# Deformable products of a convolution block: a PSUM bank of the general ring for each half band, in place of a bank of their own

## The chip, the cores and the metric

One core of one Trainium2 chip. The metric is the device time of one execution, in microseconds (us). Engines: TensorE (PE, with its weight loads PEld), VectorE (DVE), ScalarE (ACT), GpSimd (POOL) and SyncE (SP). TensorE writes only to PSUM, which this kernel uses as eight banks of 512 fp32 numbers per partition. Each engine works through its own queue in the order that the compiler wrote; an instruction that waits for a semaphore holds all that stand behind it.

## The reference, cut to what matters

Two layers run on 32 images of 96 channels, 56 x 56, all in fp32.

```python
# layer 0: inverted residual
h = silu(bn(conv1x1(x, w1)))             # 96 -> 576
h = silu(bn(depthwise3x3(h, w2)))
s = squeeze_excite(h)
x = x + bn(conv1x1(h * s, w3))           # 576 -> 96
# layer 1
ca, sa = ...                             # gates from |rfft2(x)|, channel sums
y = x * ca * sa
aux = concat([y, coord, resized |rfft2(y)|])
offset = conv3x3(aux, off_w)             # 9 taps, 2 numbers each
gate = sigmoid(conv1x1(relu(conv3x3(aux, dg1_w)), dg2_w))
y_base = conv3x3(y, base_w)
sampled = bilinear samples of y at 9 shifted points of each pixel
y_def = einsum('bcthw,oct->bohw', sampled, def_w) + def_b
z = (1 - gate) * y_base + gate * y_def
out = relu(batch_norm(z) + x)            # statistics over all images
```

## The kernel before

All weights stay on the chip. The hidden layer of one image, the attention (two spectra by matrix products) of the next, and the deformable convolution of a third are interleaved. The deformable part sets the pace: it goes by bands of 8 rows (7 bands an image, 224 in all), each band in two halves of 28 columns, and the function `layers` writes the three streams into one list of steps. A counter `slot` advances at each `pump()`, 17 slots a band. The streams `second` (attention) and `first` (hidden layer) are advanced in proportion to the slots, and the list `later` holds closures with the slot at which they are due. A scheduler then orders each engine's instructions from this program (SP's order is the program's own), and it also decides which buffer of a pool each tile gets and whose release it has to wait for.

One half of a band, in its order: `sample_tiles` forms the samples by matmuls (L739) from transposed blocks `yt` and from weights `wc`; ACT copies them to `v` (L743) and `pack` moves part of them (L750). Three slots into the next half, `end_half` calls `deform`, which sums seven products per half (L758) into PSUM. `weights` multiplies `wc` by `wr` on DVE (L710), both loaded by DMA through SP. `block_channels` makes `yt`: POOL copies blocks (L721), PE transposes them (L725), ACT copies them out (L727).

Before, both halves of a band go into one bank `pd`, from a pool of one buffer. Two slots after the second half `join` calls `combine`, four DVE operations on the whole band: L797 reads `pd` into `z` (with the bias added and the base convolution `yb` subtracted), L798 and L799 blend with the gate, L800 takes the statistics. Seven slots later `store` writes `z` to memory through POOL's queue (L1061). The pool of `z` has two buffers.

All other matmul results go to banks of the ring `mm`, six buffers, by `bank(p)`: the expansion of the hidden layer (L169, read by ACT L173), the projection (L329, L335), the spectra (L396 and L420; DVE reads squares from the ring in L379), the joint convolution of offsets, gate and base (L615, read by ACT L635, L637 and by DVE L664 into `at`), the rest of the base convolution (L644), the gate (L781), the transposes (L725) and the samples (L739). Small matrices of the attention (L440 and others) go to a bank `acc`. On DVE the hidden layer's depthwise taps (L260, L262, one instruction per tap on a half image) take most of the time; it also weights the rows that are loaded for the deformable part (L602) and reduces the spectra (L437).

```python
# L965
pools(tc, ctx, p, PSUM, (("mm", 6), ("acc", 1), ("pd", 1)))
```

Of the kernel before, what the change touches and what calls it, by code (L numbers as in the profile page):

```python
# [7 lines left out]
FP = mybir.dt.float32  # L8
I32 = mybir.dt.int32
AF = mybir.ActivationFunctionType  # L10
ALU = mybir.AluOpType
AX = mybir.AxisListType
PSUM = bass.MemoryType.PSUM
# [3 lines left out]
C, H, W = 96, 56, 56  # L17
# [3 lines left out]
RB = 8  # L21
# [14 lines left out]
BW = NBW  # L36
# [81 lines left out]
def bank(p):  # L118
    return p["mm"].tile([128, 512], FP, name="mm")


def hidden_constants(tc, ctx, a, p):

    nc = tc.nc
    cp = ctx.enter_context(tc.tile_pool(name="l0c", bufs=1))
    w = p["w0"] = {}
    for name, shape in (("w1", [C, HID]), ("w2", [128, NCH, 9]), ("w3", [128, NCH, C])):
        w[name] = cp.tile(shape, FP, name=name)
        nc.sync.dma_start(w[name], a[name + "L"])
    for name in ("sew1", "seb1", "sew2", "seb2"):  # L130
        w[name] = cp.tile(list(a[name].shape), FP, name=name)
        nc.scalar.dma_start(w[name], a[name])
    for name, parts in (("w1", C), ("w2", 128), ("w3", 128)):
        with tc.tile_pool(name=f"fq{name}", bufs=1) as tp:
            fake_quant(nc, tp, w[name], parts, name)
    with tc.tile_pool(name="l0v", bufs=1) as tp:
        vec = tp.tile([128, 8, NCH], FP, name="vec")
        nc.scalar.dma_start(vec, a["hidvec"])
        vec3 = tp.tile([C, 4], FP, name="vec3")
        nc.scalar.dma_start(vec3, a["bn3"])  # L140
        for n, v in ((1, vec[:, :4]), (2, vec[:, 4:]), (3, vec3.unsqueeze(2))):
            inv, sh = bn_affine(nc, tp, v[:, 0], v[:, 1], v[:, 2], v[:, 3], n)
            for key, t in ((f"inv{n}", inv), (f"sh{n}", sh)):
                w[key] = cp.tile(list(t.shape), FP, name=key)
                nc.vector.tensor_copy(w[key], t)

    p["hp"] = [cp.tile([128, HH + 2, WP], FP, name=f"hp{i}") for i in range(2)]
    for t in p["hp"]:
        nc.gpsimd.memset(t, 0.0)
    p["n_hp"] = 0  # L150
# [458 lines left out]
def conv3(nc, out, weights, yp, channels, j):  # L609

    view = out.rearrange("p (h w) -> p h w", h=RB)
    for k in range(NTAP):
        dy, dx = divmod(k, 3)
        r0 = j * RB + dy + PD - 1
        nc.tensor.matmul(view, weights[:, k], yp[:channels, r0 : r0 + RB, dx + PD - 1 : dx + PD - 1 + W],  # L615
                         start=(k == 0), stop=(k == NTAP - 1))
# [135 lines left out]

def deform(nc, p, pd, v, h):

    out = pd[:C, :BW].rearrange("c (q w) -> c q w", q=RB)[:, :, h * W // 2 : (h + 1) * W // 2]
    for k in range(KA):
        ks = slice(0, 128 if k else C)
        nc.tensor.matmul(out.rearrange("c q (t x) -> c t q x", x=TS), p["w"]["def"][ks, k],  # L758
                         v[ks, k].rearrange("c t s (r x) -> c t (s r) x", r=TS),
                         start=(k == 0), stop=(k == KA - 1))  # L760


def gate_of(nc, p, hid):

    pg = bank(p)
    nc.tensor.matmul(pg[:C, :BW], p["w"]["dg2"], hid, start=True, stop=True)
    return gate_from(nc, p, pg)


def gate_from(nc, p, pg):  # L770
    gate = p["q1"].tile([C, BW], FP, name="gate")
    nc.scalar.activation(gate, pg[:C, :BW], AF.Tanh, bias=p["w"]["half"]("dg2_b", C), scale=0.5)
    return gate
# [11 lines left out]
def base_conv(nc, p, j, yp):  # L785

    pb = bank(p)
    conv3(nc, pb[:C, :BW], p["w"]["base"], yp, C, j)
    yb = p["q1"].tile([C, BW], FP, name="yb")
    nc.scalar.activation(yb, pb[:C, :BW], AF.Identity, bias=p["w"]["cv"]("base_b"))  # L790
    return yb


def combine(nc, p, j, pd, yb, gate, st):

    z = p["q2"].tile([C, BW], FP, name="z")
    nc.vector.scalar_tensor_tensor(z, pd[:C, :BW], p["w"]["cv"]("def_b"), yb, ALU.add, ALU.subtract)  # L797
    nc.vector.scalar_tensor_tensor(z, gate, 1.0, z, ALU.add, ALU.mult)  # L798
    nc.vector.scalar_tensor_tensor(z, z, 0.5, yb, ALU.mult, ALU.add)  # L799
    nc.vector.bn_stats(st[:, j], z)  # L800
    return z
# [146 lines left out]
def pools(tc, ctx, p, space, sizes):  # L948
    for name, bufs in sizes:
        kw = {"space": space} if space else {}  # L950
        p[name] = ctx.enter_context(tc.tile_pool(name=f"l1{name}", bufs=bufs, **kw))


def layers(tc, a, dp, x1d, zd, stats, far):
# [6 lines left out]
    nc = tc.nc  # L961
    B = x1d.shape[0]
    with ExitStack() as ctx:
        p = {"tc": tc, "dp": ctx.enter_context(tc.tile_pool(name="l1d", bufs=3, space=DRAM))}
        pools(tc, ctx, p, PSUM, (("mm", 6), ("acc", 1), ("pd", 1)))  # L965
        hidden_constants(tc, ctx, a, p)
        constants(tc, ctx, a, p)
        yp, = padded(nc, p, a, 1)
# [21 lines left out]
        streams, later = [], []  # L990
        slot = 0
# [68 lines left out]
        def store(b, j, z):  # L1060
            nc.gpsimd.dma_start(zd[b][:, j * BW : (j + 1) * BW], z)  # L1061

        def join(n, pd, gate, st):
            b, j = bands[n]
            z = combine(nc, p, j, pd, ybs[n], gate, st)
            later.append((slot + 7, lambda: store(b, j, z)))
            if j == NBD - 1:
                nc.vector.bn_aggr(stats[:, b], st)

        def end_half(n, h, v, gate, st):  # L1070
            if h == 0:
                pds[n] = p["pd"].tile([128, 512], FP, name="pd")
            deform(nc, p, pds[n], v, h)
            if h:
                pd = pds.pop(n)
                later.append((slot + 2, lambda: join(n, pd, gate, st)))

        ends, pds = [], {}

        def fill():  # L1080
            for r in range(RB, H + 1, RB):
# [7 lines left out]
        hids, gates, ybs, hds, ready = [], [], [], [], []  # L1089
# [31 lines left out]
        for n, (b, j) in enumerate(bands):  # L1121
            if j == 0:
                st = p["st"].tile([C, NBD, 6], FP, name="st")
# [7 lines left out]
            for h in range(2):  # L1131
                v = p["vp"].tile([128, NTAP, NTH, 2, TP], FP, name="v")
# [19 lines left out]
                if h == 0:  # L1152
                    if n % 2 == 0:
                        gates.extend(gates_of(nc, p, hids[n // 2]))
                    gate = gates.pop(0)
# [108 lines left out]
def gather_block(tc, a, dp, x1d, zd, stats):  # L1264

    nc = tc.nc
    B = x1d.shape[0]
    sd = dp.tile([B, C, 2], FP, name="sd")
    with ExitStack() as ctx:
        p = {"dp": ctx.enter_context(tc.tile_pool(name="l1d", bufs=1, space=DRAM))}  # L1270
        pools(tc, ctx, p, PSUM, (("mm", 7), ("acc", 1)))
        constants(tc, ctx, a, p, True)
        yp, = padded(nc, p, a, 1)
        table = dp.tile([TAB, 4 * C], FP, name="table")
        with tc.tile_pool(name="l1z", bufs=1) as zp:
            zt = zp.tile([116, TAB * C // 116], FP, name="zt")
            nc.gpsimd.memset(zt, 0.0)
            tz = table.rearrange("(p n) f -> p (n f)", p=116)
            for i in range(4):
                nc.sync.dma_start(tz[:, i * zt.shape[1] : (i + 1) * zt.shape[1]], zt)  # L1280
        pools(tc, ctx, p, None, (("ca", 1), ("s1p", 1), ("xc", 2), ("sp", 1), ("sq", 2), ("hq", 1), ("q1", 2), ("q2", 2),
                                 ("hid", 2), ("off", 1), ("ix", 2), ("vp", 1), ("gp", 4), ("smp", 2)))
        with tc.For_i(0, B, 1) as b:
            st = p["sp"].tile([C, NBD, 6], FP, name="st")
            zo = p["dp"].tile([C, HW], FP, name="zo")
            xi = p["dp"].tile([C, HW], FP, name="xi")
            nc.sync.dma_start(xi.unsqueeze(0), x1d[bass.ds(b, 1)])
            for _ in attend(tc, p, 0, None, None, None, xi, True):
                pass
            for q in range(NB):  # L1290
                attend_table(nc, p, yp, table, xi, q)
            load_freq(nc, p, yp, 0, 0, H)
            for j in range(NBD):
                hid, wq, idx = locate(nc, p, yp, j)
                v = p["vp"].tile([C, NTAP, BW], FP, name="v")
                for t in range(GT):
                    sample_table(nc, p, table, wq, idx, v, t)
                pd = bank(p)
                for k in range(NTAP):
                    nc.tensor.matmul(pd[:C, :BW], p["w"]["def"][:, k], v[:, k], start=(k == 0), stop=(k == NTAP - 1))  # L1300
                z = combine(nc, p, j, pd, base_conv(nc, p, j, yp), gate_of(nc, p, hid), st)
                nc.sync.dma_start(zo[:, j * BW : (j + 1) * BW], z)
            mv = p["sp"].tile([C, 2], FP, name="mv")
            nc.vector.bn_aggr(mv, st)
            nc.sync.dma_start(zd[bass.ds(b, 1)], zo.unsqueeze(0))
            nc.sync.dma_start(sd[bass.ds(b, 1)].rearrange("o c n -> (o c) n"), mv)
    nc.sync.dma_start(stats, sd.rearrange("b c s -> c b s"))
# [209 lines left out]
```

## Time and profile before

| | |
|---|---|
| time, median of 3 runs | 9049.27 us (9045.97 to 9068.44) |
| the profiled execution | 9059.03 us, of which the profile's span is 9057.2 us |
| mean granted TensorE clock | 0.939 of full speed |
| busy: PE, PEld | 8175.3 us (90%), 5193.5 us (57%) |
| busy: DVE, ACT, POOL | 7184.4 us (79%), 5393.5 us (60%), 2902.8 us (32%) |
| DMA | 163 GB/s over the span |

Times of single instructions and of waits come from the profiled execution. A line of a group gives: source line, engine, operation, tiles written and read, shapes, count; then busy us and mean ns of one; then the idle time of the engine just before these instructions, and what ended it. A line of the waits gives: engine and line that waited, what released it, us in total, times, the longest. A line of the timeline gives start, duration, engine, line, operation, count and, in brackets, the idle time before it with its releaser. A fp32 matmul appears as two records. The last 280 us or so, a normalisation that waits for DMA, have no matmuls.

### The profile page before, as it was taken

The numbers are of one execution on the slowest core, as the hardware profiler recorded it, in microseconds if no ns is written. First come the engines' busy times: TensorE is split into PE (matmuls) and PEld (weight loads), VectorE is DVE, ScalarE is ACT, GpSimd is POOL, SyncE is SP. The second block draws the span as 40 slices with busy tenths as digits, with TensorE's granted clock in tenths as the row PEclk, the third lists the DMA queues.
The fourth block names the chain that finished last, engine by engine and source line by source line (L and its number), as shares of the span: only waits on it lengthen the run. The fifth ranks groups of instructions, "written<-read, shape, count | busy, mean of one in ns | idle before, by whom it ended". The sixth has DMA issues, their size and how long they took to land. (4 is left out here: it accounts for less than half of the span.)

```text
span 9057.2 us, 137476 instructions
## 1 busy us (share of the span) xinstructions
PE 8175.3 (90%) x52406; PEld 5193.5 (57%) x52406; DVE 7184.4 (79%) x6629; ACT 5393.5 (60%) x10486; POOL 2902.8 (32%) x2800
## 2 busy tenths in 40 slices
PE   5889999999999999999999999999999999999960
PEld 3456565665656566565656656565665655566640
DVE  7688888888888888888888888888888888888333
ACT  2356665666666666666666666666666666666553
POOL 0233333333333333333333333333333333333210
PEclk9889999999999999999999999999999999999985
DMA  2356666666666666666666666666666666666669
GB/s 82 108 142 160 163 169 165 157 154 153 163 166 171 166 157 147 158 165 164 172 161 154 159 157 168 165 174 161 154 154 160 165 166 172 166 156 144 144 188 416
DMA packets 1068758, 1486.48 MB, mean 164 GB/s; under 512 B 590191, under 2 KB 839839, under 8 KB 1055807
## 3 DMA queue, kind: packets, MB, share of 16 engines
q1 hardware_dynamic: 858995, 985.20, 46.4%
q10 hardware_dynamic: 153803, 329.80, 10.2%
q0 software_dynamic: 55296, 162.60, 6.7%
q8 instruction: 420, 6.88, 0.4%
q14 instruction: 244, 1.99, 0.1%
HBM read 1064.29 MB, written 412.65 MB: 163 GB/s over the span
## 5 line engine op out<-in xcount | busy, mean ns | idle before, releaser
L262 DVE SCALAR_TENSOR_TENSOR acch<-hp,w,acch 128x1512 f32<-128x1512 f32 (+1 forms) x2250 | 4456.4, 1981 | 141.4 <-ACT hp L173 103.8
L615 PE MATMUL mm<-yp,c_jointW 104*128 104x448 f32 x4032 | 1679.6, 568 | 10.1 <-DMA yp<-fqd 10.1
L758 PE MATMUL pd<-v,c_def 128*96 128x224 f32 (+1 forms) x6272 | 1468.8, 382 | 142.7 <-DVE z L797 115.6
L721 POOL COPY ybl<-yp 96x448 f32<-96x448 f32 x896 | 1048.3, 1198 | 1204.9 <-PE mm L725 1204.8
L758 PEld LDWEIGHTS pd<-v,c_def 128*96 128x96 f32 (+1 forms) x6272 | 1062.2, 176 | 449.8 <-issue 116.9
L615 PEld LDWEIGHTS mm<-yp,c_jointW 104*128 104x128 f32 x4032 | 776.6, 196 | 784.2 <-issue 747.4
L743 ACT COPY v<-mm 96x288 f32<-96x288 f32 (+1 forms) x2688 | 1004.3, 441 | 156.0 <-PE mm L739 109.3
L169 PE MATMUL mm<-xt,w 96*128 96x392 f32 (+3 forms) x2688 | 1058.5, 527 | 35.3 <-DMA xt<-in_x 33.1
L739 PE MATMUL mm<-wc,yt 64*96 64x144 f32 x12544 | 1056.9, 300 | 20.8 <-DVE sq L379 6.7
L739 PEld LDWEIGHTS mm<-wc,yt 64*96 64x96 f32 x12544 | 834.2, 164 | 317.3 <-issue 199.1
L173 ACT ACTIVATE hp<-mm,sh,inv 128x392 f32<-128x392 f32 (+2 forms) x1216 | 810.7, 673 | 344.8 <-PE mm L169 290.5
L710 DVE TENSOR_TENSOR wc<-wc,wr 128x1008 f32<-128x1008 f32 x448 | 566.6, 1265 | 412.5 <-DMA wr<-hd 385.1
L644 PE MATMUL mm<-yp,c_base0W 96*64 96x224 f32 x8064 | 830.1, 358 | 5.7 <-ACT hp L173 5.7
L329 PE MATMUL mm<-hq,w3s 128*96 128x392 f32 x2048 | 749.7, 510 | 63.6 <-DMA hq<-h2d 62.2
L672 POOL DMA_DIRECT2D od<-at x224 | 186.7, 834 | 1908.3 <-DVE at L664 1292.6
L750 ACT COPY v<-v 32x448 f32<-32x448 f32 x1344 | 755.1, 562 | 29.7
L727 ACT COPY yt<-mm 128x384 f32<-128x384 f32 (+1 forms) x896 | 353.9, 439 | 700.7 <-PE mm L725 699.0
L644 PEld LDWEIGHTS mm<-yp,c_base0W 96*64 96x64 f32 x8064 | 555.2, 135 | 282.7 <-issue 61.0
L635 ACT ACTIVATE hid<-mm,c_dg1b 50x448 f32<-50x448 f32 x224 | 140.8, 628 | 868.4 <-PE mm L615 858.4
L476 POOL TENSOR_TENSOR o<-o,xc 96x392 f32<-96x392 f32 x256 | 376.2, 1470 | 806.2 <-ACT o L339 804.2
L222 ACT ACTIVATE acch<-acch,sh,inv 128x1568 f32<-128x1568 f32 x288 | 488.4, 1696 | 202.8 <-DVE acch L262 176.5
L329 PEld LDWEIGHTS mm<-hq,w3s 128*96 128x96 f32 x2048 | 323.0, 166 | 395.2 <-issue 367.5
(194 smaller groups left out, 9325.3 us busy)
## 6 DMA issues: line engine op xcount, KB each, us to landing
h2d<-acch ACTq DMA_DIRECT2D x288, 784.0 KB
wc<-hd SPq DMA_DIRECT2D x896, 252.0 KB
wr<-hd SPq DMA_DIRECT2D x448, 504.0 KB
hq<-h2d SPq DMA_DIRECT2D x128, 980.0 KB
hq<-h2d SPq DMA_DIRECT2D x128, 784.0 KB
hq<-x1d SPq DMA_DIRECT2D x768, 98.0 KB
ht<-od SPq DMA_DIRECT2D x224, 252.0 KB
hd<-ho ACTq DMA_DIRECT2D x224, 252.0 KB
```

The lines of the kernel that those rows point to most:

```text
L169: nc.tensor.matmul(pt[p0 : p0 + w1.shape[1], : rows * W], w1, xts[hf][:, r0 * W : (r0 + rows) * W], start=True, stop=True)
L173: nc.scalar.activation(h1[lo:hi, row0 : row0 + rows, 1 : 1 + W], pt[lo:hi, : rows * W].rearrange("p (h w) -> p h w", h=rows), AF.Silu, bia ...
L262: nc.vector.scalar_tensor_tensor(acc[:, lo:hi], win, wk, acc[:, lo:hi], ALU.mult, ALU.add)
L329: nc.tensor.matmul(pts[half][:C, :EW], w3s[:, ch], hq, start=(i == 0), stop=False)
L615: nc.tensor.matmul(view, weights[:, k], yp[:channels, r0 : r0 + RB, dx + PD - 1 : dx + PD - 1 + W], start=(k == 0), stop=(k == NTAP - 1))
L644: nc.tensor.matmul(pb[i * BC : (i + 1) * BC, : BW // 2].rearrange("p (h w) -> p h w", h=RB // 2), w["base"][:, k], yp[:C, r0 + i * RB // 2 ...
L710: p["tc"].keep_in_program_order(nc.vector.tensor_tensor(wc, wc, wr, ALU.mult))
L721: nc.gpsimd.tensor_copy(yb[:, :, s], blocks)
L739: nc.tensor.matmul(pt[k][:C, (t - lo) * KP : (t - lo + 1) * KP], yt[ps, t], s[ps, t * KP : (t + 1) * KP], start=True, stop=True)
L743: nc.scalar.copy(v[:C, :, lo:hi, k].rearrange("c k t p -> c t k p"), pt[k][:C, : (hi - lo) * KP].rearrange("c (t k p) -> c t k p", t=hi - ...
L750: nc.scalar.copy(v[C:, 1 + 2 * i : 3 + 2 * i], v[i * QC : (i + 1) * QC, KA:])
L758: nc.tensor.matmul(out.rearrange("c q (t x) -> c t q x", x=TS), p["w"]["def"][ks, k], v[ks, k].rearrange("c t s (r x) -> c t (s r) x", r=T ...
```

## The change

Each half of a band gets a bank of its own from the ring, and the pool `pd` is gone; the ring has seven buffers. The half's products lie in the first 224 columns of that bank. Two slots after each half's products (before: after the second half's) `difference` reads it into the half's columns of `z`, so L797 is executed twice a band, on 96 x 224 elements as 8 rows of 28. The tile `z` is taken from its pool when the first half is summed. After the second half `combine` does the other three operations on the whole band as before. The fallback `gather_block`, which runs only where offsets reach too far, gets the same operation written out in its old form.

```diff
 def deform(nc, p, pd, v, h):
-    out = pd[:C, :BW].rearrange("c (q w) -> c q w", q=RB)[:, :, h * W // 2 : (h + 1) * W // 2]
+    out = pd[:C, : BW // 2].rearrange("c (q w) -> c q w", q=RB)
...
-def combine(nc, p, j, pd, yb, gate, st):
-    z = p["q2"].tile([C, BW], FP, name="z")
-    nc.vector.scalar_tensor_tensor(z, pd[:C, :BW], p["w"]["cv"]("def_b"), yb, ALU.add, ALU.subtract)
+def difference(nc, p, h, pd, yb, z):
+    half = lambda t: t.rearrange("c (q w) -> c q w", q=RB)[:, :, h * W // 2 : (h + 1) * W // 2]
+    nc.vector.scalar_tensor_tensor(half(z), pd[:C, : BW // 2].rearrange("c (q w) -> c q w", q=RB), p["w"]["cv"]("def_b"),
+                                   half(yb), ALU.add, ALU.subtract)
+
+def combine(nc, p, j, z, yb, gate, st):
     nc.vector.scalar_tensor_tensor(z, gate, 1.0, z, ALU.add, ALU.mult)
     nc.vector.scalar_tensor_tensor(z, z, 0.5, yb, ALU.mult, ALU.add)
     nc.vector.bn_stats(st[:, j], z)
...
-        pools(tc, ctx, p, PSUM, (("mm", 6), ("acc", 1), ("pd", 1)))
+        pools(tc, ctx, p, PSUM, (("mm", 7), ("acc", 1)))
...
-        def join(n, pd, gate, st):
+        def join(n, h, pd, z, gate, st):
             b, j = bands[n]
-            z = combine(nc, p, j, pd, ybs[n], gate, st)
+            difference(nc, p, h, pd, ybs[n], z)
+            if not h:
+                return
+            combine(nc, p, j, z, ybs[n], gate, st)
             later.append((slot + 7, lambda: store(b, j, z)))
...
         def end_half(n, h, v, gate, st):
+            pd = bank(p)
+            deform(nc, p, pd, v, h)
             if h == 0:
-                pds[n] = p["pd"].tile([128, 512], FP, name="pd")
-            deform(nc, p, pds[n], v, h)
-            if h:
-                pd = pds.pop(n)
-                later.append((slot + 2, lambda: join(n, pd, gate, st)))
-        ends, pds = [], {}
+                zs[n] = p["q2"].tile([C, BW], FP, name="z")
+            z = zs.pop(n) if h else zs[n]
+            later.append((slot + 2, lambda: join(n, h, pd, z, gate, st)))
+        ends, zs = [], {}
```

## The prediction, made before the changed kernel ran

> **What bounds the kernel now.** I read the page's engine line and slices first, then busy time by stage, then the waits, then the timeline at the waits that matter. One image takes about 266 us in the steady part; this is the stage line of one image, 3960 to 4227 us (busy time of PE, PEld, DVE, ACT, POOL, then the granted clock):
>
> ```profile
> PE 8175.3 (90%) x52406; PEld 5193.5 (57%) x52406; DVE 7184.4 (79%) x6629; ACT 5393.5 (60%) x10486; POOL 2902.8 (32%) x2800
> 3960.00:4227.00 267.00, 251.99 (x1627) 160.07 (x1626) 223.66 (x198) 165.72 (x325) 90.33 (x88) 0.96 0.65 160
> ```
>
> PE is busy for 252 of 267 us, DVE for 224. So PE sets the time, and what lengthens it is its idle time (15 us an image) and the half-rate clock. Matmuls stand in one queue in compiled order: a wait of one holds all. The waits over the whole run say what ends that idle time:
>
> ```profile
> PE pd L758 <- DVE z L797: 115.6, 26, 6.1
> PE acc L440 <- DVE m_fy L437: 72.8, 30, 5.6
> PE acc L440 <- DVE m_fe L437: 71.1, 31, 2.5
> PE mm L725 <- DVE at L664: 57.2, 28, 5.7
> ```
>
> The first is the one that the change speaks of: the deformable products (L758) wait until VectorE has read `pd`. It happens once an image, at its last band. DVE's and PE's timelines there:
>
> ```profile
> 3956.58 1.53 DVE L710 TENSOR_TENSOR wc<-wc,wr 128x1008 f32<-128x1008 f32 x1 [3.47 <-DMA wr<-hd]
> 3958.03 6.09 DVE L262 SCALAR_TENSOR_TENSOR acch<-hp,w,acch 128x1568 f32<-128x1568 f32 x3
> 3964.15 0.68 DVE L797 SCALAR_TENSOR_TENSOR z<-pd,c_cvec,yb 96x448 f32<-96x448 f32 x1
> ...
> 3959.21 0.93 PE L169 MATMUL mm<-xt,w 96*128 96x392 f32 x2
> 3964.98 1.03 PE L758 MATMUL pd<-v,c_def 96*96 96x224 f32 x2 [4.84 <-DVE z L797]
> ```
>
> DVE lost 3.47 us to a weight transfer, then ran three tap operations of the other image, and only then came to `z`. The read is late because DVE's own queue is late, not because it is long. The clock after such a wait (the last figures of a stage line are clock, DMA share, GB/s):
>
> ```profile
> 3960.00:3966.00 6.00, 1.16 (x5) 0.82 (x5) 5.80 (x7) 3.89 (x8) 0.58 (x1) 0.80 0.98 283
> 3966.00:3972.00 6.00, 6.00 (x22) 4.63 (x21) 4.42 (x7) 1.27 (x3) 1.58 (x3) 0.50 1.05 192
> ```
>
> Between 500 and 8500 us the trace has 115 half-rate stretches, 737 us together (6.4 us each, so 3.2 us of PE work lost each). 32 of them, 232 us, follow a wait of L758.
>
> **Part 1: one DVE read becomes two.** Rows of DVE operations with a PSUM or short operand:
>
> ```profile
> L797 DVE SCALAR_TENSOR_TENSOR z<-pd,c_cvec,yb 96x448 f32<-96x448 f32 x224 | 152.2, 679 | 170.3 <-PE pd L758 166.1
> L922 DVE SCALAR_TENSOR_TENSOR thT<-shift,c_svec,thT 56x56 f32<-56x56 f32 x42 | 10.9, 259 | 0.0
> ```
>
> A line through 56 elements at 259 ns and 448 at 679 gives 439 ns for 224. Two halves cost 878 ns, +199 ns a band, x224 = +45 us of DVE. It is bounded by 0 and by 2 x 679 - 679 = 152 us. DVE idles some 43 us an image, so this is hidden as work; without that cover it would be the whole +45. Matmul count and sizes (7 a half, 379 ns a pass), ACT, POOL and SP lists are the same: no cost. The `z` buffer is taken 12 slots earlier and so waits for the store of two bands before; set against the trace that store lands at least 9 us before, mostly 43 us: nothing. The gather branch, also edited, has no instruction in the trace: nothing.
>
> **Part 2: the wait that goes.** With no `pd` buffer, L758 no longer waits for L797: at most 115.6 us of idle time, plus half of 232 us at half rate = 116.
>
> **Part 3: what is late next.** The half's bank now belongs to the ring, and stays taken from the products until DVE reaches the half: two slots and then DVE's lag. Whichever matmul is compiled onto that bank next waits for DVE, and everything behind it in PE's queue waits too. I took the compiled order of the changed kernel with its waits, and gave each instruction the time that its twin has in the trace of before (the half: the end of the DVE instruction ahead of it, plus 0.44 us). The wait is DVE's time less PE's arrival. The same reckoning on the kernel before gives 357 us between 500 and 8500 us, with 122 us for L758 against 115.6 in the whole run by the profile, so the method reads the old waits rightly. For the changed kernel, by place within an image (us from its end; 30 images):
>
> - Image end: L758's wait does not vanish. The second gate matmul (L781), or a sampling matmul (L739), some three groups ahead of L758, now takes the bank of that same late half. PE meets it about 2 us earlier, DVE is no earlier. 122 becomes 171: +50.
> - At 37: matmuls that take banks DVE reads in L379 and in a half; about 2.6 us an image = 81 when waits that follow at once are counted once. In the order L440 (m_fe, at 54) now stands behind three matmuls of L615, and its 68 us go. With 11 of before: about 0.
> - At 112 to 123, in the second transform: 256, where before has 6: +250. This is the largest. Its mechanism in one image: L169 at 4082.29 takes the bank of a first half that stands in DVE's queue behind the first L262 of the next unit:
>
> ```profile
> 4082.29 0.93 PE L169 MATMUL mm<-xt,w 96*128 96x448 f32 x2
> ...
> 4086.96 1.03 DVE L260 TENSOR_SCALAR acch<-hp,w 128x1568 f32<-128x1568 f32 x1
> 4088.02 3.93 DVE L262 SCALAR_TENSOR_TENSOR acch<-hp,w,acch 128x1568 f32<-128x1568 f32 x1
> ```
>
>  The half would end at 4092.4: L169, and the FFT matmuls behind it, wait 9.9 us. Before, DVE's lag here cost nothing, as no bank hung on it. Alternate images have 5 to 7 and 7 to 13 us.
> - At 145 to 160 (L725 on `at`, L440 on m_fy): 135 becomes 125; as PE arrives late from the place before, the `at` part (53) mostly goes: -50.
> - At 189 and 231 (projection and sampling matmuls behind w3s, a half, and a half behind a wc that waits for DMA): 141, before 3. I take half, +70, because DVE's wait there is for a transfer that a later PE also moves.
>
> Of the 250 I take 205: the transfer wait of L602 (1.4 us an image) is not PE's to repeat. Idle time: 50 + 0 + 205 - 50 + 70 = +275. Bounds: with every wait kept in full 905 - 357 = +548; if waits within 40 us of each other absorb each other fully, 499 - 291 = +208.
>
> Clock: the places at 123 (30 images) and 231 (15) are new waits of over 2 us; 37 takes the place of 54, the image end stays. 45 stretches x 3.2 us = +145. Bounds: 11 more waits over 1.5 us (absorbed) and 63 (full), times 737 / 94 waits x 1/2 = 3.9 us: +43 and +246.
>
> [...] The trace: 28 waits for m_fe, of about 2.4 us, are each followed by half rate, 154 us together. [...]
>
> Sum: 275 + 145 = +420. The profiled execution took 9059.0 us (span 9057.2), 9.8 above the median of 9049.3: 9059 + 420 = 9479 as profiled, 9470 as a median. What lies within 0.3% (27 us) of before I count as no change.
>
> **The rivals.**
> A (my forecast, 0.70): waits move onto the ring and mostly add; 9250 to 9700.
> B (faster, 0.05): no ring matmul meets a late half, since DVE, with halves offered earlier, is ahead of PE. Then 115.6 + 116 are gained: 9049 - 232 = 8817. It decides if the lag at 123 falls below zero from 9.9 and 5.4 us. Against it: DVE's queue has the same operations before the half, and 45 us more.
> C (slower, little, 0.13): a stall early in an image lets DVE catch up, so later ones shrink below my bound: half of the +208, 104, plus 43: about 9200. For it: DVE has 43 us of idle time an image. Against it: much of that idle time is DVE waiting for ACT's hp, which PE feeds, so DVE stops as well when PE stops.
> D (slower, much, 0.10): all add: 548 + 246: 9843.
> E (no change, 0.02): C's losses equal B's gain.
>
> The range 9220 to 9750 holds A, and the near ends of C and D. Faster 0.05, same 0.02, slower 0.93.
>
> **What would show it.** Right: no L758 on L797; new rows of PE waiting for L797 at L169, L396, L739 and L781, 350 to 650 us together; more half-rate time, a mean clock of 0.92 to 0.93 against 0.939; PE's busy time up by the clock alone; L797 448 times at about 440 ns. Wrong: PE's waits for z below 150 us in all, or DVE with no idle time left (then it has become the bound, and Part 1's cover is gone).

## The result and the profile after

The changed kernel takes 9450.61 us (median of 4 runs, 9422.1 to 9474.71) against 9051.45 us for the kernel before on the same chip (4 runs): a ratio of 1.0436, with a 95% interval of 1.0401 to 1.0472. The forecast was 9470 us. Its profiled execution, from which the lines below come, took 9422.1 us.

The head of the page of the changed kernel; the second line gives busy time, share of the span and instructions:

```profile
span 9420.3 us, 137589 instructions
...
PE 8320.5 (88%) x52406; PEld 5277.8 (56%) x52406; DVE 7108.3 (75%) x6853; ACT 5399.9 (57%) x10486; POOL 3029.6 (32%) x2800
```

The number of matmuls is the same (52406 records in either trace, all of which write PSUM tiles: `mm`, `acc` and, before, `pd`), yet PE is busy 145 us longer: the mean granted clock fell from 0.939 to 0.924. The other part is idle time. Between the first and the last matmul record TensorE is idle 551 us before and 769 us after, +218. 145 + 218 = 363 us, which is the growth of the span (9057.2 to 9420.3). DVE, with 224 more instructions, is busy a little less. So nothing here is more work: the loss is waiting and the clock that the waiting costs.

The waits of PE in the changed kernel (us in total, times, longest), its largest eight without two that come once a run:

```profile
PE mm L615 <- DMA yp<-fqd: 149.8, 30, 6.3
PE mm L739 <- DVE z L797: 127.9, 31, 6.7
PE acc L440 <- DVE m_fe L437: 71.6, 32, 3.7
PE mm L169 <- DVE z L797: 67.4, 29, 6.2
PE mm L781 <- DVE z L797: 64.0, 13, 7.0
...
PE mm L725 <- POOL ybl L721: 37.4, 11, 5.2
PE mm L329 <- DMA hq<-h2d: 37.2, 16, 4.7
PE mm L396 <- DVE z L797: 36.1, 14, 3.9
```

Three things are to be read in it. L758 no longer waits for `z` (115.6 us before, 0.8 us now). In its place L739, L169, L781, L396 and, with 15 us in smaller lines, L615, L420 and L329 do: 310 us together. And the first line is new in size: L615 waits 149.8 us for the row of the spectrum (`fqd` to `yp`), 10.1 us before. Against that L440's wait for `m_fy` (72.8 us before) has only 6.8 us left, and L725's for `at` (57.2 us) is gone.

One of the waits for a half, in the timeline (start, duration, engine, line, operation, count, in brackets the idle time before it). First TensorE:

```profile
3794.35 2.81 PE L758 MATMUL mm<-v,c_def 96*96 96x224 f32 x14
...
3799.68 0.99 PE L781 MATMUL mm<-hid,dg2p 50*96 50x448 f32 x2
3807.72 1.06 PE L781 MATMUL mm<-hid,dg2p 50*96 50x448 f32 x1 [7.05 <-DVE z L797]
```

and VectorE in the same stretch:

```profile
3800.24 1.41 DVE L710 TENSOR_TENSOR wc<-wc,wr 128x1008 f32<-128x1008 f32 x1 [4.70 <-DMA wr<-hd]
3801.57 5.61 DVE L262 SCALAR_TENSOR_TENSOR acch<-hp,w,acch 128x1568 f32<-128x1568 f32 x3
3807.22 0.45 DVE L797 SCALAR_TENSOR_TENSOR z<-mm,c_cvec,yb 96x224 f32<-96x224 f32 x1
```

The products were done at about 3797. VectorE had first lost 4.70 us to a weight transfer and then ran three taps of the other image that stand ahead of the read in its queue. The gate matmul, which has nothing to do with that half, took the next turn of its bank and waited 7.05 us; so did all behind it (no matmul record begins between the L781 at 3799.68, which took 0.99 us, and the one at 3807.72). This is the picture of the prediction's first example with another matmul in the place of L758. Counted by time alone, 107 idle stretches of TensorE over 0.5 us, 350 us together, ended within 0.3 us of the end of an L797; VectorE was busy for 301 us of them, 215 in L262 and 47 in the reads themselves.

The new wait of L615 has another cause. The same place in one image, before:

```profile
3051.35 0.41 PE L582 MATMUL acc<-fy,c_rows 29*56 29x56 f32 x4
3051.79 4.57 PE L758 MATMUL pd<-v,c_def 96*96 96x224 f32 x14
...
3058.98 2.73 PE L758 MATMUL pd<-v,c_def 96*96 96x224 f32 x12 [0.40 <-ACT v L743]
3061.86 1.38 PE L615 MATMUL mm<-yp,c_jointW 104*128 104x448 f32 x3 [0.15 <-DMA yp<-fqd]
```

and after:

```profile
3128.13 0.41 PE L582 MATMUL acc<-fy,c_rows 29*56 29x56 f32 x4
3128.47 2.89 PE L758 MATMUL mm<-v,c_def 96*96 96x224 f32 x14
...
3138.19 9.06 PE L615 MATMUL mm<-yp,c_jointW 104*128 104x448 f32 x18 [4.61 <-DMA yp<-fqd]
```

L582 makes the row; ACT copies it, POOL's queue writes it to memory, SP's queue loads it into `yp`; then L615 can start. From the end of L582 to the start of L615 the median is 10.5 us before and 10.4 us after. Before, TensorE had work for that time: fourteen records of L758, for the most part at half rate (4.57 us here at a mean granted clock of 0.63; 4.74 us at 0.63 are the medians over the images), and, ahead of L615, twelve more, six of the seven products of the next half. That second half already had its bank. In the changed kernel it needs one of the ring, whose turn comes after L615's, and the compiled order has all seven products behind L615. Twelve records of cover (2.7 us) are gone, the first fourteen run at full rate (2.89 instead of 4.57 us, a granted clock of 1.00), and what is left of the chain shows as a wait. The fourteen traces divide in this way. Where the second half has its bank early (the kernel before with or without the tap, the split read, the whole band in the ring, and banks of their own), nearly every image has 26 or 28 records of L758 between L582 and L615, and the wait is 1 to 38 us in all. Where each half takes a bank of the ring, it has 14, and the wait is 116 to 150 us, or 61 and 90 us in the two kernels that load an old row.

### The profile page after: what moved, and what is told of

It reads as the page before. It is cut to its first block, busy times and chain, and to the rows that moved or that the text cites. A ratio compares the mean times of both kernels' runs of the same rounds, so it can differ in the third digit from the quotient of the medians.

```text
span 9420.3 us, 137589 instructions
## 1 busy us (share of the span) xinstructions
PE 8320.5 (88%) x52406; PEld 5277.8 (56%) x52406; DVE 7108.3 (75%) x6853; ACT 5399.9 (57%) x10486; POOL 3029.6 (32%) x2800
## 5 line engine op out<-in xcount | busy, mean ns | idle before, releaser
L262 DVE SCALAR_TENSOR_TENSOR acch<-hp,w,acch 128x1512 f32<-128x1512 f32 (+1 forms) x2250 | 4355.6, 1936 | 127.6 <-ACT hp L173 96.9
L615 PE MATMUL mm<-yp,c_jointW 104*128 104x448 f32 x4032 | 1748.3, 585 | 164.6 <-DMA yp<-fqd 149.8
L721 POOL COPY ybl<-yp 96x448 f32<-96x448 f32 x896 | 1177.7, 1341 | 1608.0 <-PE mm L725 1607.9
L758 PE MATMUL mm<-v,c_def 128*96 128x224 f32 (+1 forms) x6272 | 1386.8, 370 | 20.3 <-ACT v L750 17.9
L615 PEld LDWEIGHTS mm<-yp,c_jointW 104*128 104x128 f32 x4032 | 797.4, 203 | 955.5 <-issue 768.9
L739 PE MATMUL mm<-wc,yt 64*96 64x144 f32 x12544 | 1120.7, 304 | 146.5 <-DVE z L797 127.9
L758 PEld LDWEIGHTS mm<-v,c_def 128*96 128x96 f32 (+1 forms) x6272 | 1034.6, 170 | 322.3 <-issue 84.1
L169 PE MATMUL mm<-xt,w 96*128 96x392 f32 (+3 forms) x2688 | 1089.9, 540 | 100.5 <-DVE z L797 67.4
L739 PEld LDWEIGHTS mm<-wc,yt 64*96 64x96 f32 x12544 | 876.5, 166 | 455.2 <-issue 190.3
L710 DVE TENSOR_TENSOR wc<-wc,wr 128x1008 f32<-128x1008 f32 x448 | 590.5, 1318 | 391.3 <-DMA wr<-hd 378.5
L329 PE MATMUL mm<-hq,w3s 128*96 128x392 f32 x2048 | 771.3, 522 | 40.8 <-DMA hq<-h2d 37.2
L644 PEld LDWEIGHTS mm<-yp,c_base0W 96*64 96x64 f32 x8064 | 551.3, 134 | 275.8 <-issue 67.4
L476 POOL TENSOR_TENSOR o<-o,xc 96x392 f32<-96x392 f32 x256 | 343.9, 1343 | 860.3 <-ACT o L339 858.3
L169 PEld LDWEIGHTS mm<-xt,w 96*128 96x128 f32 (+1 forms) x2688 | 369.6, 181 | 399.7 <-issue 219.9
```

Source lines behind the costliest of these rows:

```text
L169: nc.tensor.matmul(pt[p0 : p0 + w1.shape[1], : rows * W], w1, xts[hf][:, r0 * W : (r0 + rows) * W], start=True, stop=True)
L262: nc.vector.scalar_tensor_tensor(acc[:, lo:hi], win, wk, acc[:, lo:hi], ALU.mult, ALU.add)
L329: nc.tensor.matmul(pts[half][:C, :EW], w3s[:, ch], hq, start=(i == 0), stop=False)
L644: nc.tensor.matmul(pb[i * BC : (i + 1) * BC, : BW // 2].rearrange("p (h w) -> p h w", h=RB // 2), w["base"][:, k], yp[:C, r0 + i * RB // 2 ...
L710: p["tc"].keep_in_program_order(nc.vector.tensor_tensor(wc, wc, wr, ALU.mult))
L721: nc.gpsimd.tensor_copy(yb[:, :, s], blocks)
```

## The experiments

Ratios are against the kernel before on the same chip in the same session; for the twelve experiments its medians were 9033 to 9034 us, and 9051 us is the session of the changed kernel. "z" is TensorE's waiting for the read of the products, "fqd" L615's waiting for the row.

| kernel | time, us | ratio, 95% interval | z, us | fqd, us | clock |
|---|---|---|---|---|---|
| before | 9051 | 1 | 115.6 | 10.1 | 0.939 |
| changed | 9451 | 1.0436 [1.0401, 1.0472] | 310 | 149.8 | 0.924 |
| split read | 9026 | 0.9995 [0.9982, 1.0009] | 108.9 | 5.9 | 0.938 |
| ring of 7, whole band | 9139 | 1.0118 [1.0100, 1.0137] | 196.7 | 32.9 | 0.937 |
| two own banks, halves | 8943 | 0.9902 [0.9883, 0.9921] | 0 | 12.1 | 0.954 |
| ring of 7, ACT reads halves | 9112 | 1.0084 [1.0064, 1.0104] | 0 | 138.0 | 0.943 |
| changed, old row | 9359 | 1.0369 [1.0350, 1.0389] | 298 | 89.8 | 0.926 |
| ACT reads halves, old row | 8991 | 0.9947 [0.9927, 0.9968] | 0 | 61.1 | 0.945 |
| own bank, ACT reads band | 8957 | 0.9920 [0.9904, 0.9937] | 0 | 16.3 | 0.949 |
| two own banks, whole band | 8999 | 0.9959 [0.9946, 0.9972] | 0 | 13.5 | 0.949 |
| before, a tap less | 9100 | 1.0076 [1.0057, 1.0095] | 46.4 | 37.8 | 0.940 |
| changed, a tap less | 9408 | 1.0410 [1.0386, 1.0434] | 301 | 143.7 | 0.926 |
| changed, ring of 6 | 9340 | 1.0340 [1.0320, 1.0360] | 345 | 116.2 | 0.936 |
| halves of one own bank | 9044 | 1.0014 [1.0004, 1.0023] | 185.4 | 1.2 | 0.941 |

**The read alone, in two.** The kernel before, with

```diff
-    nc.vector.scalar_tensor_tensor(z, pd[:C, :BW], ..., yb, ALU.add, ALU.subtract)
+    for h in range(2):
+        half = lambda t: t.rearrange("c (q w) -> c q w", q=RB)[:, :, h * W // 2 : (h + 1) * W // 2]
+        nc.vector.scalar_tensor_tensor(half(z), half(pd[:C, :BW]), ..., half(yb), ALU.add, ALU.subtract)
```

> The kernel before, with its own bank for a band, but VectorE takes that bank in two reads of 28 columns, back to back, where it took it in one. Theory (the loss is TensorE waiting, through a bank of the ring, for VectorE's late queue; the extra read as such is hidden): 9050 to 9110 us, about 45 us more VectorE busy time, and only the one old wait of L758 for z, some 5 to 40 us larger. Rival 1 (the extra VectorE instruction and its fixed cost are the loss): 9250 us or more. Rival 2 (a ring of seven banks puts TensorE's queue in a worse order, whoever reads the half): as before, 9050.

No difference: 0.9995. A half's read took 442 ns on average. The old wait is 108.9 us, a little shorter where the theory had it longer, and the time lies just below the theory's band. The 224 extra instructions of VectorE are hidden; rival 1 falls, and rival 2 stands so far.

**The ring of seven, whole bands.** The kernel before, with

```diff
-        pools(tc, ctx, p, PSUM, (("mm", 6), ("acc", 1), ("pd", 1)))
+        pools(tc, ctx, p, PSUM, (("mm", 7), ("acc", 1)))
...
-                pds[n] = p["pd"].tile([128, 512], FP, name="pd")
+                pds[n] = bank(p)
```

> Half of the change: no bank of its own, a ring of seven, but the whole band stays in one bank of the ring and is read once, as before the change. Theory: 9120 to 9350 us; the wait of L758 for z is gone, and matmuls that take the next turn of that bank (L739, L781, L396) wait for z, 150 to 300 us together, since a reckoning from the compiled order and the times of before gives 219 us for them; fewer places an image than with halves. Rival 1 (extra read): 9050, as there is only one read. Rival 2 (order of a ring of seven): about the changed kernel's 9450, with the wait of L615 for its DMA (150 us in the changed kernel) still there.

+1.18%, in the theory's band. The waits of this kernel:

```profile
PE mm L739 <- DVE z L797: 99.0, 26, 7.3
PE mm L781 <- DVE z L797: 97.7, 30, 7.0
...
PE mm L615 <- DMA yp<-fqd: 32.9, 15, 4.1
```

The old wait of L758 has moved whole to the matmuls that take the bank next, and grown from 115.6 to 196.7 us. With one bank a band that is about all; L169 and L396 do not appear, since no first half hands a bank back alone.

**Halves in two banks of their own.** The changed kernel, with

```diff
-        pools(tc, ctx, p, PSUM, (("mm", 7), ("acc", 1)))
+        pools(tc, ctx, p, PSUM, (("mm", 5), ("acc", 1), ("pd", 2)))
...
-            pd = bank(p)
+            pd = p["pd"].tile([128, 512], FP, name="pd")
```

> The changed kernel, its halves read as there, but each half has a bank of a pool of two and the ring keeps five. Theory: 9050 to 9250 us; no matmul of the ring waits for z, L758 may (some 10 to 80 us), and waits for a ring of five are new: the reckoning has 154 us of L169 waiting for VectorE's L664. Rival 1 (extra read): about 9450. Rival 2 (order of the ring): unclear in time, but the wait of L615 for its DMA would be near 10 us, as the ring isn't seven.

The reads, their number and the eight banks are as in the changed kernel. Where the halves lie differs, and with it the length of the ring; the time is 8943 us: below the theory's band, and 5.1% below the changed kernel (0.9902 / 1.0436 = 0.949). Its waits:

```profile
PE mm L169 <- DVE at L664: 58.8, 15, 7.1
...
PE mm L739 <- DVE sq L379: 47.4, 21, 6.1
...
PE mm L615 <- DMA yp<-fqd: 12.1, 16, 1.5
```

Nothing waits for `z`, not even L758. The wait for `at` through the shorter ring is the one expected new wait, 59 us where the reckoning had 154. In this order six products stand ahead of L615 again, and the row is covered. That is also what rival 2 had said of the row, so this kernel alone does not divide the theory from rival 2; the next one does.

**ScalarE reads the halves.** The changed kernel, with

```diff
-    nc.vector.scalar_tensor_tensor(half(z), pd[...], p["w"]["cv"]("def_b"), half(yb), ALU.add, ALU.subtract)
+    nc.scalar.activation(half(z), pd[...], AF.Identity, bias=p["w"]["cv"]("def_b"))
...
+            nc.vector.tensor_tensor(z, z, ybs[n], ALU.subtract)
             combine(nc, p, j, z, ybs[n], gate, st)
```

> The changed kernel with the ring of seven and the halves in it, but ScalarE takes each half (adding the bias) out of PSUM into z, and VectorE subtracts the base convolution afterwards from SBUF, once a band. Nothing of VectorE's queue hangs on a ring bank of a half any more. Theory: 8950 to 9150 us, no wait of TensorE for z above 10 us in all, the clock back at 0.935 or more; the wait of L615 for its DMA falls back below 60 us if it followed from the waits for z. Rival 1 (number of VectorE instructions): 9400, as VectorE does as many per band as before plus one. Rival 2 (order of a ring of seven): 9250 or more, with the wait of L615 for its DMA still at about 150.

The ring is the changed kernel's, and no matmul waits for `z`: 9112 us, 3.4% below the changed kernel. As far as one pair can tell, that is what VectorE's place in the hand-back costs; `m_fy` is waited for again (76.4 us against 6.8), so the rest is not all equal. (The expectation miscounts in rival 1: VectorE has four instructions a band here, one fewer than in the changed kernel, so this run says nothing on it; the split read does.) But the wait of L615 did not fall:

```profile
PE mm L615 <- DMA yp<-fqd: 138.0, 30, 8.7
PE acc L440 <- DVE m_fe L437: 78.1, 31, 6.1
PE acc L440 <- DVE m_fy L437: 76.4, 31, 7.6
```

So it does not follow from the waits for `z`: rival 2 is right on the row, the theory on the time. The compiled order around L615 is the changed kernel's, all seven products behind it. This is the second cause, and the next two kernels try to put a price on it.

**The row made early.** In `load_freq`, in the changed kernel and in the one where ScalarE reads the halves:

```diff
-    nc.sync.dma_start(yp[...], p["fq", b][:, r0:r1])
+    nc.sync.dma_start(yp[...], p["fq", max(b - 1, 0)][:, r0:r1])
```

> The changed kernel in its own order of instructions, but the row of the spectrum that goes into yp is that of the image before (for the first image its own); this leaves out that an image uses its own spectrum. The transfer fqd to yp has then long been possible when L615 comes, so the wait of L615 for it, 150 us in the changed kernel and followed by 222 us at half rate, must go, and all else stays. Theory, as it stands after the first four kernels (two causes: matmuls on ring banks wait for VectorE, and once an image six deformable products that covered this transfer are compiled behind L615): 9150 to 9330 us, with the waits for z at 300 us or a little more. Rival 1 (the waits for z are all of the loss; the wait of L615 only shows a delay that is there anyway): 9400 to 9450. Rival 2 (the transfer is the whole loss): below 9100.

> The kernel in which ScalarE takes the halves out of the ring (9112 us, 138 us of L615 waiting for fqd to yp, and no wait for z), with the spectrum's row of the image before; this leaves out that an image uses its own. Both causes are then gone. Theory: 8860 to 9000 us, below the kernel before, as its old wait of L758 is gone too. Rival (ScalarE's extra 127 us of work, or other waits of a ring of seven, are what keep that kernel slow): 9080 to 9120.

The changed kernel gains 0.6% by it, less than the theory's band (9150 to 9330) and more than rival 1 allows. The mistake was to think that the transfer would be over because it was allowed to be. In one image it was issued at 3106.29 us, its last signal came at 3116.89 and L615 started at 3117.03; over the images the last signal came a median of 10.9 us after the issue, against 2.3 us in the changed kernel, and 89.8 us of the wait remain. What did go was paid in full: 60 us less waiting, and 72 us less half-rate time behind it (222 to 150), half of which is 36, make 96 us; the span of the profiled execution fell by 85. With ScalarE reading, the same edit gives 1.4% and the kernel falls below the one before, as the theory said (8991). So the row costs 0.6% in the one and 1.4% in the other, and not all of its wait was taken away here.

**Two cures that leave the ring of six or five.** The kernel before, its own bank, with ScalarE's read of the whole band and a subtraction by VectorE:

```diff
-    nc.vector.scalar_tensor_tensor(z, pd[:C, :BW], p["w"]["cv"]("def_b"), yb, ALU.add, ALU.subtract)
+    nc.scalar.activation(z, pd[:C, :BW], AF.Identity, bias=p["w"]["cv"]("def_b"))
+    nc.vector.tensor_tensor(z, z, yb, ALU.subtract)
```

> The kernel before with its own bank for a band and its ring of six; ScalarE takes the bank into z (with the bias) and VectorE then subtracts the base convolution from SBUF. Nothing of VectorE's queue hangs on a bank of products. Theory: the 115 us of L758 waiting for z go, the order of L615 stays as before, 8850 to 8960 us; the transfer fqd to yp then sets L615 in part of the images (20 to 80 us). Rival 1 (that transfer takes the whole place of the wait): 9000 to 9050. Rival 2 (ScalarE becomes late for v and L173): slower than 9050.

And the kernel before with `(("mm", 5), ("acc", 1), ("pd", 2))` and nothing else:

> The kernel before with two banks of their own for whole bands and a ring of five; one read a band. Against the halves in two banks of their own (8943 us) this tells what the halves themselves give. Theory: no wait of L758 for z; L169 waits for VectorE's L664 through the ring of five (about 59 us there, reckoned 154), and L440 still waits for m_fy (72 us before, none with halves read by VectorE): 8980 to 9090 us. Rival (the second bank alone is the gain, halves do nothing): 8930 to 8950, with no wait for m_fy.

Both are faster than before (0.9920 and 0.9959): the old wait of L758 was worth removing, and is removed by a prompt reader or by a second bank of its own. In the second, the time fell in the band but for a reason that I had not given: the wait for `m_fy` is nearly gone there too (8.0 us). In 13 images TensorE now waits for `at` (67.8 us, at L169) a little earlier, and comes to L440 later; why `m_fy` is in time in the other images was not followed up. Against the halves in two banks (8943 us) this leaves 0.6% for taking halves, no more than a new compiled order alone can be worth (see the ring of six below).

**A tap less.** In both kernels the eighth of VectorE's nine taps is left out, by `elif k != 7:` in place of `else:` ahead of L262.

> The kernel before with one of VectorE's nine depthwise taps left out (the eighth, k = 7), some 280 operations of 1.93 us, about 17 us of VectorE an image; it is the control of the next. Theory (TensorE's waits come from VectorE's queue being late): waits for z, at, m_fe and m_fy, 317 us together, fall by half or more, 8700 to 8930 us. Rival (lateness is set by transfers and by TensorE itself): above 8990.

> The changed kernel with the same tap left out. The banks, the ring and the number of reads are as in the changed kernel; only VectorE is less late. Theory: TensorE's waits for z, 310 us, fall below 150; the time to 8800 to 9100 us, at most 2.5% above the one without the tap from the kernel before (4.4% with all taps); the wait of L615 for fqd, which does not hang on VectorE, stays above 80 us. Rival (the order of TensorE's queue is the loss): 4% above that control or more.

Both miss in time. VectorE's busy time fell by 571 us in the kernel before (7184.4 to 6613.2) and by 536 us in the changed one (7108.3 to 6571.9). In the kernel before, the four waits did fall by about half, 317 to 164 us (`z` 115.6 to 46.4), and yet it became 0.8% slower, as its rival had it: a wait of L566 for `sa` (95.6 us, 7.6 before) came instead, and those for `fqd` and `v` grew. In the changed kernel z is still 301 us, at other matmuls:

```profile
PE mm L169 <- DVE z L797: 125.6, 30, 7.3
PE mm L739 <- DVE z L797: 81.6, 30, 7.6
PE mm L396 <- DVE z L797: 75.8, 19, 6.7
```

The ratio of the two, 1.033, lies between the theory's 1.025 and the rival's 1.04. So in the changed kernel the waits for a half did not shrink with the amount of VectorE's work, where in the kernel before those for the band did. What stands ahead of the read in VectorE's queue fills them still: counted by time alone as above, VectorE was busy for 287 of 334 us in this kernel, 165 in L262 and 59 in L710. Leaving an operation out gave a new compiled order on every engine, so this pair does not tell more than that.

**A ring of six, and the halves of one bank.** The changed kernel with `("mm", 6)`, one bank unused; and the kernel of two own banks with ring six and, in place of the second bank, `pd = both[:, 256 * h : 256 * (h + 1)]` of one bank `both`:

> The changed kernel with a ring of six (one bank left unused). Each bank comes round a seventh sooner, so more matmuls meet a half that VectorE has not reached. Theory: 9550 to 9800 us, waits for z 380 to 550 us together (the reckoning adds about 190 us of waits to the changed kernel's). Rival (a half bank blocks the same places whatever the length of the ring): 9400 to 9480.

> Halves read as in the changed kernel, ring of six as before; the two halves of a band lie in the two halves (256 columns each) of one bank of their own, so no second bank is needed. In the compiled program a half's products wait for the read of the half just before. Theory: no ring matmul waits for z, L758 does, 110 to 180 us (reckoned 179, the kernel before 122); 9000 to 9130 us. Rival (taking halves early is itself the gain of the two own banks, 8943 us): 8930 to 8960.

The ring of six went the wrong way for the theory: more waiting for `z` (345 us, and L739 meets a half twice an image instead of once), but 9340 us, 1% below the ring of seven and below the rival's band too. Idle time is 747 us against 769; the waits for `m_fe` are shorter (45.7 us instead of 71.6) and half rate follows 1 of 32 of them instead of 27 of 32, and PE's busy time is 8268.0 instead of 8320.5 us. Here a shorter ring was not the dearer one; which matmul of which stage comes to stand behind a half, in the order that results, seems to count for more, but no run here varies that by itself. The halves of one bank gave the old kernel's time with 185.4 us at L758, as reckoned (179): taking halves early was no gain here, where the next half must wait for the read.

## Why the prediction was right, point by point

**Bound and cover.** PE sets the time in both kernels; Part 1 holds. A half's read took 436 ns (predicted 439) and L797's total rose by 43 us (45):

```profile
L797 DVE SCALAR_TENSOR_TENSOR z<-mm,c_cvec,yb 96x224 f32<-96x224 f32 x448 | 195.3, 436 | 482.7 <-PE mm L758 478.7
```

The split read alone cost nothing.

**Part 2.** The wait of L758 went. The prediction credits it with 115.6 us of idle time and 116 of clock; of the 232 us at half rate behind the latter, 201 follow a wait for `z`, the rest L758's waits for `v`. The kernels with a prompt reader or a second bank show 37 to 90 us of gain in all, since the next late thing (`m_fy`, `m_fe`, `sq`, `at`) shows as soon as it is gone.

**Part 3, by place.** The prediction's reckoning, made again with the changed kernel's own times (500 to 8850 us, 30 images), gives for the image end 139 us (predicted 171), at 37 and 54 together 77 (predicted 81), at 112 to 123 105 (predicted 256, 205 taken), at 145 to 165 5 (85 left after its -50), at 189 and 231 81 (141, of which 70 were taken). The signs hold. The term most mis-sized is the one at 112 to 123, too large by 100 us; the next is the one at 145 to 165, where the waits for `m_fy` went as well as those for `at` (6.8 us left of 72.8), 80 us more than the prediction let go. At 112 to 123 the waits of L169 are 2.3 us on average (67.4 / 29), not 5 to 10: TensorE, delayed earlier in the image, comes later, and VectorE has moved on meanwhile. That is rival C's mechanism, at these two places. The `m_fe` wait at 54, which the prediction let go, stayed (71.6 us).

**What the sum lacked.** By the waits, those for VectorE changed by 310 - 115.6 for `z` and by 7.0 - 130.0 for `m_fy` and `at` together: +71 us net, where the places summed to +275 (bounds +208 to +548). What made up the rest had no term in the sum: the row's wait at L615, +140 us, and L725's for POOL's copies (`ybl`), +36, against -25 at L329 (`hq`). Together +222, and +218 was measured as idle time. The reckoning weighed only waits for VectorE and ScalarE in the new order and no chain of DMAs, though that order showed the seven products behind L615. So the forecast of the idle time (+275) was near because these two terms came out too high and another was missing; the sign and the mechanism were right, and that part of the accuracy was luck.

**Clock.** +145 forecast, and PE's busy time grew by 145.2. The price per stretch that the rows gave held: half-rate time grew by 317 us over the run, half of which is 159, with 44 stretches more (125 to 169). By the largest wait in the 7 us ahead of each stretch, 45 more follow a wait for `z` (26 before, 71 after), the number that the forecast had. But 27 more follow the row's wait at L615 (1 before, 28 after), which had no term, and 27 fewer the waits for `m_fy` and `at` (29 before, 2 after), of which the forecast dropped none; these two nearly cancel, 218 us against 205 at half rate, and that is luck again. The last section tells which lengths of wait were followed by half rate.

**Rivals.** B (faster) falls: VectorE is not ahead at these places. D falls: the waits do absorb each other in part. A held, C in two places. "What would show it" said 350 to 650 us of waits for `z`; it is 310, below that band and well over the 150 that would have spoken against the mechanism.

**What stays open.** How the 4.4% divides. Taking VectorE out of the hand-back, in the same order around L615, gives back 3.4%; the old row 0.6% or 1.4%, with 61 to 90 us of that wait left. At the rate at which it paid in the changed kernel (85 us of the span for 60 us of waiting) the 140 us that the row's wait grew by would be worth some 200 us, an estimate. These do not add up to a clean account, since each edit changes the compiled order, and the ring of six shows that such an order alone can be worth 1%. Taking VectorE out of the hand-back also brings back a wait for `m_fy` that the changed kernel had lost. Why the waits for `m_fe` are 1.4 us in some orders and about 2.3 us in others wasn't followed up.

## What to carry to other kernels

A bank that joined the ring here was given back by its reader, and users of the ring then waited for that reader's queue (310 us at seven lines with VectorE as the reader, none with ScalarE); give a ring only to banks whose reader is prompt, and keep a slow reader's bank apart (here two banks of its own and a ring of five beat one and six, and seven without). When a wait is to be removed, look for what was covered by the same stretch of work, transfers too: matmuls that need no new bank had been covering a chain of two DMAs (10.5 us from L582 to L615). The best version of this study is the halves in two banks of their own, 0.990 of the kernel before; ScalarE's read of the whole band, 0.992, has an interval that overlaps with its own.

## What the runs showed of the hardware

The clock fell after most waits of 2.0 to 2.5 us, and after few of up to 1.5 us. In the fourteen traces I took TensorE's idle stretches (500 to 8500 us) with no other idle time over 0.1 us and no half-rate stretch within 7 us ahead, and no other idle time within 7 us behind, and looked whether a half-rate stretch began by 7 us after. Up to 1.5 us: 60 of 1036; 1.5 to 2.0 us: 144 of 252; 2.0 to 2.5 us: 408 of 506; 2.5 to 3.25 us: 212 of 236; above that all 512. The stretches, at a granted clock of 0.50, lasted 3.41, 6.83 or 10.24 us for the most part (107 of the 115 in the kernel before and 140 of the 148 in the changed one, 500 to 8500 us), steps of 3.41 us. A wait of up to 1.5 us was thus nearly free of the clock's price, and one of 2.0 to 2.5 us was followed four times in five by a stretch that costs about 3 us (28 waits for `m_fe` in the kernel before were followed by 154 us at half rate, about half of which is lost: the fourteen records of L758 behind L582 took 2.89 us at a granted clock of 1.00 and 5.54 us at 0.50 in that kernel). This is part of why nearly the same idle time cost less in the ring of six than in the ring of seven (waits for `m_fe` of 1.4 us on average, 1 of 32 followed by half rate, against 2.2 us and 27 of 32).

A transfer that was allowed early was not done early. In the kernel with the old row L606 was issued 10.7 us ahead of L615's start, in the changed kernel 2.4 us (3135.78 to 3138.19), and TensorE waited in both, as the transfer took 10.6 us in the one and 2.3 us in the other. With the old row it was issued just behind loads of `wc`, `wr`, `ht` and `x1d` (3102.97 to 3105.67), and the DMA engines were 90% busy or more in five of the six slices of 0.7 us from 3106.1 to 3110.3, and 60% or more in the other; in the changed kernel SP held it for 10 us after them. That these loads are what slowed it is likely, not shown.
